# Base products of batches 2 and 3 taken as one seven-block product in the setup, and base and x remainders added by adding loads

## The chip, the cores and the metric

The kernel runs on one core of a Trainium2 chip. A core has five engines that work side by side, each on its own queue of instructions, in order: TensorE (PE in the profile) multiplies matrices, VectorE (DVE), ScalarE (ACT) and GpSimd (POOL) work elementwise, SyncE (SP) here only issues DMAs; ACT and POOL issue DMAs too. Engines wait for one another through semaphores. SBUF is the on-chip memory; PSUM holds what PE writes. The metric is device time in microseconds (us), lower is better, as the median of several executions.

## The reference, cut to what matters

There are 8 batches b, each of 1024 rows x of width 512. From cond, a low-rank update of the weights of layer 0 is computed (rank 8), and from weight, ys and d a modulated weight of layer 1:

```python
xw = gelu(layernorm(cond) @ w1 + b1) @ w2 + b2          # 8 x 8192
x_a, x_b = split(xw)                                     # 512 x 8 each, per batch
layer = base_layer + x_a @ x_b.T                         # per batch
x = x + (x + x @ layer)                                  # layer 0, with its residuals
ys = cond * scale; d = rsqrt((ys*ys) @ (w*w) + eps)      # per batch
out = x + ((x * ys) @ weight) * d                        # layer 1, with its residual
```

Both layers are linear in x, so the kernel multiplies x once by one 512x512 matrix per batch,

P(b) = (2 I + layer) @ N(b), with N(b) = I + diag(ys) weight diag(d).

The part (2 I + base) @ N(b) is called the base product; the rank term is added to it later.

## The kernel before

**Precision.** Products are made in fp32r, and each operand is held as a rounded part h and a remainder l (value minus h). A product takes three matmuls, h·h, h·l and l·h. Making a pair takes one ACT cast (`round_right`, L344; `round_b`, `split_p`, `split_x`) and one DVE subtraction (`rest`, L350), the latter after the former. ACT and DVE run through the helper at L62, so nearly all their profile lines say L62; all matmuls say L45, transposes L48. One reads the profile by tile names: nh and nl are the parts of N, bh and bl those of 2 I + base (held transposed), ph and pl those of P, xs those of x.

**Setup (to about 80 us).** While 16 MB of w2 stream in on SP's queue, PE multiplies each 1 MB tile by the gelu rows (`w2_group`, L389; products px), and between these fills itself with base products. N is made in halves of 256 rows by `n_half` (L333, DVE: per 128 rows one scale pass, and one small add of I on the diagonal block). Batch 0's base product is summed while weights arrive (`first_base`); those of batches 1, 2 and 3 are made by `Base` (L524): 16 steps of three matmuls for each of 4 row blocks' k chunks, so 48 matmuls of 128x512 for a batch, copied from PSUM to q by ACT. `Fill` (L695) runs these three one after another; `fill.make_n`, `fill.round` and `fill.finish` make, cast and subtract a half of N.

Between lie the rank steps: when px_1 is complete, `rank_t` (L435) makes `by`, transposes it (pb), multiplies it by the weight (pt_t) and selects rows with `stack` (L418; ps_t, then st_t). When px_0 is complete, `split(with_bias(0))` and `stack` make st_a from ps_a in the same way. P of batch 0 gets four rank products `rank_first` (L497; pr), which DVE adds to q_0, and `split_p` makes ph and pl of it.

**base itself.** base, transposed and with 2 I, lies in b_raw as the stationary operand. Batch 0's product is made with diag(ys) weight alone, without the I of N and without d; it is scaled by d first (`times_d`), so base, loaded as b_nat (1 MB, SP's queue), gets 2 I on its diagonal (`twice_i_plus_base`, L476) and is added to q_0 in four DVE passes (`add_base`, L481).

**Main stage (from about 80 us).** For batches 0 to 5, `main` (L811) multiplies 128 rows of x by P: 12 matmuls into po, copied and stored by ACT. Batches 4 and 5, and 6 and 7, get their base products in this stage as pairs (`Pair`, L547): with N's halves written [N1(b), N1(b+1); N2(b), N2(b+1)], a two-batch product of 2x2 blocks takes seven block products instead of eight (Strassen's scheme in Winograd's form; block p has right sums by `sums`, L562, and left operands from `left_sum`, L368, sums of b_raw's quarters). A `unit` (L611) is six matmuls, one of two row blocks of one p. Batches 6 and 7 use a like scheme for x (`Seven`).

**Order.** PE's matmuls are pinned to program order (L45). In the setup DVE, ACT and SP are pinned too (`InOrder`, L52, until `InOrder.on = False`), so the program text is the queue of each engine. In the main stage they are free, and a scheduler orders them.

**Buffers.** `big` has nine tiles of 1 MB for w2, x, q, b_raw, b_nat, the left sums' tile sraw and the xs; a load into one waits until the last reader of the tile that held it is done. nh and nl have two buffers each, n has four, and acc, the PSUM banks of base products, four.

The last part of the setup's text in the kernel before, with the order of the steps that the prediction follows:

```python
    fill.round(3, 0)
    fill.units(4)
    done = stack(xa, neg_a, "a", 0)
    fill.finish(3, 0)
    sa[0] = done()
    fill.units(3)
```

Of the kernel before, what the change touches and what calls it, by code (L numbers as in the profile page):

```python
# [7 lines left out]
F32 = mybir.dt.float32  # L8
F32R = mybir.dt.float32r
AF = mybir.ActivationFunctionType  # L10
ALU = mybir.AluOpType
# [19 lines left out]
def cond_resid_kernel(ctx: ExitStack, tc: tile.TileContext, small, cond, condrows, consts,  # L31
# [20 lines left out]
    class InOrder:  # L52
# [4 lines left out]
        def __init__(self, engine):  # L57
            self.engine = engine
# [20 lines left out]
    def big_tile(name, dtype=F32):  # L79
        return big.tile([P, KC, D], dtype, tag="big", name=name)  # L80
# [252 lines left out]
    def n_half(b, j):  # L333

        n = npool.tile([P, 2, D], F32, tag="n", name=f"n_{b}_{j}", bufs=4)
        for kk in range(2):
            k = 2 * j + kk
            ve.scalar_tensor_tensor(n[:, kk, :], w_sb[:, k, :], ysT[:, k, b:b + 1],
                                           d_all[b], ALU.mult, ALU.mult)
            blk = n[:, kk, k * P:(k + 1) * P]  # L340
            ve.tensor_add(blk, blk, ident)
        return n

    def round_right(n, name, wide=True):  # L344
# [20 lines left out]
    a11, a21 = b_raw[:, 0:2, 0:HD], b_raw[:, 0:2, HD:D]  # L365
    a12, a22 = b_raw[:, 2:4, 0:HD], b_raw[:, 2:4, HD:D]

    def left_sum(i):  # L368
        if i == 5:
            sraw["s"] = big_tile("sraw").rearrange("p k (u i) -> p k u i", u=2)  # L370
        s1, s2, s3, s4 = (sraw["s"][:, u] for u in range(4))
        s, x, y, op = {5: (s1, a21, a22, ve.tensor_add), 6: (s2, s1, a11, ve.tensor_sub),
                       3: (s4, a12, s2, ve.tensor_sub), 7: (s3, a11, a21, ve.tensor_sub)}[i]
        op(s, x, y)
        h = cp.tile([P, 2, HD], F32R, name=f"sh_{i}")
        l = cp.tile([P, 2, HD], F32R, name=f"sl_{i}")
        se.copy(h, s)
        ve.tensor_sub(l, s, h.bitcast(F32))
        left[i] = h, l

    b_nat = []


    px = [xps.tile([P, D], F32, name=f"px_{h}") for h in range(2)]
# [100 lines left out]
    def round_w(k):  # L485
        se.copy(wh[:, k, :], w_sb[:, k, :])
# [37 lines left out]
    class Base:  # L524
# [21 lines left out]

    class Pair:  # L547
# [144 lines left out]
    bcast_d(0)  # L692
    first_base(3, (1, 2, 3))

    class Fill:  # L695


        def __init__(self):
            self.bases = [Base(b) for b in (1, 2, 3)]
            self.ns, self.rests = {}, {}  # L700

        def units(self, count):
            for _ in range(count):
                if self.bases[0].at == 4 * KC:
                    self.bases.pop(0)
                self.bases[0].units(1)

        def make_n(self, b, j):
            self.ns[b, j] = n_half(b, j)

        def round(self, b, j):
            self.rests[b, j] = round_right(self.ns[b, j], f"{b}_{j}", b == 3)

        def finish(self, b, j):
            next(f for f in self.bases if f.b == b).add(self.rests[b, j]())

    fill = Fill()
    fill.make_n(1, 0)
    fill.round(1, 0)
    fill.make_n(1, 1)  # L720
    keep_first((0, 1))
    fill.round(1, 1)
    keep_first((2, 3))
    fill.finish(1, 0)
    for c in range(2):
        times_d(0, c)
    fill.finish(1, 1)
# [6 lines left out]
    fill.units(4)  # L734
    for k in range(2, KC):
        rest_w(k)
    fill.make_n(2, 0)
    w2_group()
    w2_group()
    fill.units(4)  # L740
    fill.round(2, 0)
    fill.make_n(2, 1)
    fill.finish(2, 0)
    w2_group()
    w2_group()
    fill.units(6)
    w2_group()
    steps = rank_t()
    next(steps)
    w2_group()  # L750
    next(steps)
    fill.units(4)
    w2_group()
    next(steps)
    w2_group()
    fill.units(2)
    fill.round(2, 1)
    next(steps)
    fill.finish(2, 1)
    next(steps)  # L760
    fill.units(3)
    twice_i_plus_base()
    w2_group()
    next(steps)
    w2_group()
    next(steps)
    mask_t()
    add_base(0)
    fill.units(2)
    fill.make_n(3, 0)  # L770
    next(steps)
    w2_group()
    w2_group()
    next(steps)
    fill.units(2)
    w2_group()
    load_x(0, 0)
    xa = (split(with_bias(0)),)
    fill.round(3, 0)
    fill.units(4)  # L780
    done = stack(xa, neg_a, "a", 0)
    fill.finish(3, 0)
    sa[0] = done()
    fill.units(3)
    fill.make_n(3, 1)
    p_tiles(0)
    rank_first(0)
    rank_first(1)
    fill.round(3, 1)
    fill.units(2)  # L790
    split_p(0, 0, 0)
    rank_first(2)
    rank_first(3)
    split_p(0, 0, 1)
    fill.finish(3, 1)
    split_p(0, 1)
    split_x(0, 0)
    fill.units(4)
    sa[1] = stack(xa, neg_a, "a", 1)()
    left_sum(5)  # L800
    fill.units(8)
    split_x(0, 1)
    for p in (6, 3, 7):
        left_sum(p)
    InOrder.on = False

    setup.close()
# [284 lines left out]
```

## Time and profile before

| | us |
|---|---|
| median of 3 executions | 302.23 (301.96 to 302.74) |
| profiled execution | 302.08 |
| its span | 300.3 |
| PE busy | 293.4 (98%), 1501 instructions |
| DVE busy | 211.0 (70%) |
| ACT busy | 154.1 (51%) |
| POOL busy | 34.8 (12%) |
| DMA | 62.14 MB, mean 207 GB/s |

The span is the time from the first to the last recorded instruction of one profiled execution; the device time has 1.8 us around it. The page divides the span into 40 slices of 7.5 us. A group's line gives engine, operation, output<-inputs, partitions x elements, count, busy time and mean, then the idle time ahead of it and what ended that. "PEld" is the load of a stationary operand, beside PE's matmuls. Matmuls are pipelined: one of 128x512 is recorded with about 0.39 us, but 12 in a row take 2.72 to 2.80 us in the chain that ended last. In timelines, a line is start, duration, engine, operation and tiles.

### The profile page before, as it was taken

Reading aid. Unit: us, or ns where it says so; the run is one execution under the profiler, and the core shown is the slowest. Engines: PE = TensorE matmul, PEld = TensorE weight load, DVE = VectorE, ACT = ScalarE, POOL = GpSimd, SP = SyncE. Lnnn points to the kernel's source line nnn. Section 1 sums busy time; section 2 is a strip of 40 time slices with the busy share of each in tenths; the row PEclk is TensorE's granted clock in tenths of the full one; section 3 lists DMA queues with packets and bytes.
Section 4 is the critical chain, followed back from the end, with each engine's and each line's share of the span. In section 5 each row is a group of like instructions: output and inputs, shape, how many; then the busy total and the mean of one; then the engine's idle time right before and its main releaser. Section 6 shows DMA issues by size and latency. Waiting matters only on the chain.

```text
span 300.3 us, 4005 instructions
## 1 busy us (share of the span) xinstructions
PE 293.4 (98%) x1501; PEld 227.1 (76%) x1501; DVE 211.0 (70%) x312; ACT 154.1 (51%) x226; POOL 34.8 (12%) x74
## 2 busy tenths in 40 slices
PE   7999999999999999999999999999999999999995
PEld 2655465466877778888887888888778888998995
DVE  4779840979569999935869994366562996479722
ACT  4757132256566673647634463656442663663630
POOL 0011000057004551000003600000000000000000
PEclk9999999999999999999999999999999999999999
DMA  7999999696619984605513841524516785131234
GB/s 210 410 428 419 405 424 419 219 326 183 197 70 305 306 288 126 239 35 210 204 43 97 230 164 46 201 55 192 210 70 210 244 267 227 38 140 49 93 140 142
DMA packets 19524, 62.14 MB, mean 207 GB/s; under 512 B 2720, under 2 KB 4000, under 8 KB 15152
## 3 DMA queue, kind: packets, MB, share of 16 engines
q1 hardware_dynamic: 6896, 39.57, 35.7%
q10 hardware_dynamic: 8832, 15.99, 14.2%
q0 software_dynamic: 3776, 6.31, 8.0%
q8 instruction: 12, 0.20, 0.3%
q14 instruction: 8, 0.07, 0.1%
HBM read 44.02 MB, written 17.84 MB: 206 GB/s over the span
## 4 chain that ended last, share of the span: by engine, by line
PE 84%; DVE 9%; ACT 3%; DMA 2%; issue 1%; SPq 0%; ACTq 0%
PE po L45 44%; PE pp L45 13%; PE pq L45 10%; PE sw L45 5%; PE px L45 4%; PE sz L45 2%; PE pg L45 2%; DVE n L62 2%; DMA b_raw<-in_baseT 2%; DVE sraw L62 1%; PE pr L45 1%; PE sv L45 1%; ACT o L62 1%; DVE sl L62 1%; ACT sh L62 1%
## 5 line engine op out<-in xcount | busy, mean ns | idle before, releaser
L45 PE MATMUL po<-ph,xs 128*128 128x512 f32 x384 | 123.8, 392 | 0.0
L45 PEld LDWEIGHTS po<-ph,xs 128*128 128x128 f32 x384 | 72.1, 188 | 16.8 <-issue 1.7
L45 PE MATMUL po<-pl,xs 128*128 128x512 f32 x192 | 74.8, 389 | 0.0
L62 ACT COPY o<-po 128x512 f32<-128x512 f32 x48 | 28.1, 586 | 52.8 <-PE po L45 52.8
L45 PEld LDWEIGHTS po<-pl,xs 128*128 128x128 f32 x192 | 36.1, 188 | 7.4
L62 DVE TENSOR_TENSOR xs<-x,xs 128x1024 fp32r<-128x1024 f32 x24 | 29.0, 1221 | 10.5 <-ACT xs L62 10.4
L62 ACT CAST xs<-x 128x1024 fp32r<-128x1024 f32 x24 | 24.9, 1052 | 3.7 <-DMA x<-in_x 1.9
L62 DVE TENSOR_TENSOR nl_p<-n,nh_p 128x1024 fp32r<-128x1024 f32 x14 | 17.1, 1222 | 12.3 <-ACT nh_p L62 12.2
L62 DVE TENSOR_TENSOR pl<-q,ph 128x1024 fp32r<-128x1024 f32 (+1 forms) x16 | 18.3, 1153 | 6.2 <-ACT ph L62 6.1
L62 DVE TENSOR_TENSOR q<-pr,q 128x512 f32<-128x512 f32 x32 | 20.1, 682 | 3.5 <-PE pr L45 3.5
L511 POOL DMA_DIRECT2D fa<-kept_a x28 | 13.7, 502 | 64.9 <-PE pr L45 64.8
L45 PE MATMUL pq<-nh,bh 128*128 128x512 f32 x48 | 19.8, 412 | 0.0
L45 PE MATMUL pq<-nl,bh 128*128 128x512 f32 x48 | 19.1, 398 | 0.1
L45 PE MATMUL pq<-nh,bl 128*128 128x512 f32 x48 | 19.0, 395 | 0.0
L62 DVE SCALAR_TENSOR_TENSOR n<-w_sb,ysT,d 128x512 f32<-128x512 f32 x24 | 17.7, 745 | 1.2 <-DMA d<-d_out 1.2
L62 ACT CAST nh_p<-n 128x1024 fp32r<-128x1024 f32 x14 | 14.8, 1054 | 6.3 <-PE pp L45 5.5
L62 ACT COPY o<-sw 128x512 f32<-128x512 f32 (+1 forms) x15 | 7.5, 500 | 19.2 <-PE sw L45 14.4
L62 ACT CAST ph<-q 128x1024 fp32r<-128x1024 f32 (+1 forms) x16 | 15.8, 1001 | 1.2 <-DVE q L62 0.8
L45 PE MATMUL px<-w,hT 128*32 128x512 f32 x128 | 16.0, 601 | 0.0
L62 ACT COPY q<-pp 128x512 f32<-128x512 f32 x20 | 11.7, 587 | 7.7 <-PE pp L45 7.7
L45 PEld LDWEIGHTS pq<-nh,bh 128*128 128x128 f32 x48 | 9.0, 188 | 8.4 <-issue 5.0
L511 POOL DMA_DIRECT2D ft<-kept_t x28 | 13.8, 509 | 5.2 <-DMA kept_t<-st_t 5.0
(185 smaller groups left out, 515.1 us busy)
## 6 DMA issues: line engine op xcount, KB each, us to landing
w<-in_w SPq DMA_DIRECT2D x16, 1024.0 KB, 10.5
x<-in_x SPq DMA_DIRECT2D x16, 1024.0 KB, 5.4
out<-o ACTq DMA_DIRECT2D x48, 256.0 KB, 3.2
out<-o ACTq DMA_DIRECT2D x6, 512.0 KB, 2.9
ft<-kept_t POOLq DMA_DIRECT2D x28, 64.0 KB, 3.4
fa<-kept_a POOLq DMA_DIRECT2D x28, 64.0 KB, 2.9
d<-d_out POOLq DMA_DIRECT2D x6, 256.0 KB, 5.2
w_sb<-in_weight SPq DMA_DIRECT2D x2, 512.0 KB, 5.3
```

Of the source, the lines that this page charges most:

```text
L45: tc.keep_in_program_order(nc.tensor.matmul(*args, **kw))
L62: return lambda *a, **kw: pin(f(*a, **kw)) if InOrder.on else f(*a, **kw)
L511: nc.gpsimd.dma_start(fold[name, b][32 * c:32 * c + 32, :], kept[name, g][32 * i:32 * i + 32, :])
```

## The change

Base products of batches 2 and 3 are no longer two `Base` of 48 matmuls each but one `Pair(2)` of 14 units of six, in the setup. Each unit's operands are made by the same calls in program order: `make_n`, `round` (right sum on DVE, cast on ACT) and `finish` (remainder on DVE). The left sums, made at the setup's end before, are made ahead of the units that need them, in two steps (`left_raw`, sum and cast; `left_rest`, remainder); b_raw is free after them.

base is not loaded to b_nat: `add_base` adds 2 I to q_0's diagonal blocks in one DVE pass, and a DMA on POOL's queue adds base from HBM to q_0 as it writes (`accum_op`). In the same way, the remainders of batch 0's x tiles 1 to 3 are not made by DVE: ACT writes -h, and a DMA on POOL's queue adds x from HBM to it. `n_half` adds I to both diagonal blocks in one pass.

```diff
@@ n_half
-            blk = n[:, kk, k * P:(k + 1) * P]
-            ve.tensor_add(blk, blk, ident)
+        blk = n.rearrange("p k (c i) -> p (k c) i", i=P)[:, 2 * j:2 * j + 6:5, :]
+        ve.tensor_add(blk, blk, ident.unsqueeze(1).to_broadcast([P, 2, P]))
@@ left sums
-    def left_sum(i):
+    def left_raw(i):
...
         h = cp.tile([P, 2, HD], F32R, name=f"sh_{i}")
+        se.copy(h, s)
+        sraw[i] = s, h
+
+    def left_rest(i):
+        s, h = sraw[i]
         l = cp.tile([P, 2, HD], F32R, name=f"sl_{i}")
-        se.copy(h, s)
         ve.tensor_sub(l, s, h.bitcast(F32))
@@ w2_group
-        if len(todo) == 6:
-            b_nat.append(big_tile("b_nat"))
-            sy.dma_start(b_nat[0], base)
@@ base added to q_0
-    def twice_i_plus_base():
-        for c in range(KC):
-            blk = b_nat[0][:, c, c * P:(c + 1) * P]
-            ve.scalar_tensor_tensor(blk, ident, 2.0, blk, ALU.mult, ALU.add)
-
-    def add_base(b):
-        for c in range(KC):
-            ve.tensor_add(q[b][:, c, :], q[b][:, c, :], b_nat[0][:, c, :])
+    def add_base():
+
+        blk = q[0].rearrange("p k (c i) -> p (k c) i", i=P)[:, 0:16:5, :]
+        ve.scalar_tensor_tensor(blk, ident.unsqueeze(1).to_broadcast([P, KC, P]), 2.0, blk,
+                                ALU.mult, ALU.add)
+        nc.gpsimd.dma_start(q[0], base, accum_op=ALU.add)
@@ split_x
-            ve.tensor_sub(xs[b, j][:, 1], t, xs[b, j][:, 0].bitcast(F32))
+            hi, lo = xs[b, j][:, 0], xs[b, j][:, 1]
+            if b == 0 and j:
+                se.mul(lo, hi.bitcast(F32), -1.0)
+                nc.gpsimd.dma_start(lo, x[b, j // 2][:, :, (j % 2) * 2 * P:(j % 2 + 1) * 2 * P],
+                                    accum_op=ALU.add)
+            else:
+                ve.tensor_sub(lo, t, hi.bitcast(F32))
```

The order of the setup's second half after the change, from the first w2 products behind base 1's first half (class `Fill` is gone; base 1 is `base1`, the pair is `two`):

```python
    two = Pair(2)
    two.make_n(1)
    w2_group(); w2_group()
    base1.units(4)
    two.round(1); two.make_n(2); two.finish(1)
    left_raw(5); left_raw(6)
    w2_group(); w2_group()
    base1.units(6)
    two.round(2); left_rest(5); left_raw(7); left_raw(3)
    w2_group(); steps = rank_t(); next(steps)      # by, and its cast
    left_rest(6)
    w2_group(); next(steps)                        # remainder of by
    left_rest(7); base1.units(2); two.finish(2); two.unit(); left_rest(3)
    w2_group(); next(steps)                        # pb
    two.make_n(5); two.round(5)
    w2_group(); two.unit(); next(steps)            # pt_t
    add_base(); two.finish(5); next(steps)
    two.units(2)
    w2_group(); next(steps); w2_group(); next(steps)
    mask_t(); two.unit(); two.make_n(6); next(steps); two.round(6)
    w2_group(); w2_group(); next(steps)
    two.unit(); two.finish(6)
    w2_group(); load_x(0, 0)
    xa = (split(with_bias(0)),)
    two.round(3); two.units(2)                     # product 6
    done = stack(xa, neg_a, "a", 0)                # ps_a0
    sa[0] = done()                                 # st_a0
    two.finish(3); two.round(7); two.unit()        # product 3, block 0
    p_tiles(0); rank_first(0); rank_first(1)
    two.unit()                                     # product 3, block 1
    split_p(0, 0, 0); rank_first(2); rank_first(3)
    split_p(0, 0, 1); split_p(0, 1)
    two.finish(7); split_x(0, 0)
    two.units(2)                                   # product 7
    two.round(4)
    sa[1] = stack(xa, neg_a, "a", 1)()
    two.finish(4); split_x(0, 1)
    two.units(2)                                   # product 4
```

(Several calls stand on one line here, and the comments on the right are the document's.)

More of the change, by code (lines that the diff above doesn't have):

```diff
@@ L375, in left_sum @@
         h = cp.tile([P, 2, HD], F32R, name=f"sh_{i}")
+        se.copy(h, s)
+        sraw[i] = s, h
+    def left_rest(i):
+        s, h = sraw[i]
         l = cp.tile([P, 2, HD], F32R, name=f"sl_{i}")
-        se.copy(h, s)
         ve.tensor_sub(l, s, h.bitcast(F32))
         left[i] = h, l
-    b_nat = []
     px = [xps.tile([P, D], F32, name=f"px_{h}") for h in range(2)]
@@ L693, in cond_resid_kernel, with round1 @@
     first_base(3, (1, 2, 3))
[L695 to L720, printed above, removed]
+    base1, n1 = Base(1), {}
+    def round1(j):
+        n1[j] = round_right(n1[j], f"1_{j}", False)
+    n1[0] = n_half(1, 0)
+    round1(0)
+    n1[1] = n_half(1, 1)
     keep_first((0, 1))
-    fill.round(1, 1)
+    round1(1)
     keep_first((2, 3))
-    fill.finish(1, 0)
+    base1.add(n1[0]())
     for c in range(2):
         times_d(0, c)
-    fill.finish(1, 1)
+    base1.add(n1[1]())
     for c in range(2, KC):
@@ L733, in cond_resid_kernel @@
         round_w(k)
-    fill.units(4)
+    base1.units(4)
     for k in range(2, KC):
         rest_w(k)
-    fill.make_n(2, 0)
+    two = Pair(2)
+    two.make_n(1)
     w2_group()
     w2_group()
[L740 to L743, printed above, removed]
+    base1.units(4)
+    two.round(1)
+    two.make_n(2)
+    two.finish(1)
+    left_raw(5)
+    left_raw(6)
     w2_group()
     w2_group()
-    fill.units(6)
+    base1.units(6)
+    two.round(2)
+    left_rest(5)
+    left_raw(7)
+    left_raw(3)
     w2_group()
@@ L749, in cond_resid_kernel @@
     next(steps)
+    left_rest(6)
     w2_group()
     next(steps)
-    fill.units(4)
+    left_rest(7)
+    base1.units(2)
+    two.finish(2)
+    two.unit()
+    left_rest(3)
     w2_group()
     next(steps)
+    two.make_n(5)
+    two.round(5)
     w2_group()
-    fill.units(2)
-    fill.round(2, 1)
+    two.unit()
     next(steps)
-    fill.finish(2, 1)
+    add_base()
+    two.finish(5)
     next(steps)
-    fill.units(3)
-    twice_i_plus_base()
+    two.units(2)
     w2_group()
@@ L767, in cond_resid_kernel @@
     mask_t()
-    add_base(0)
-    fill.units(2)
-    fill.make_n(3, 0)
+    two.unit()
+    two.make_n(6)
     next(steps)
+    two.round(6)
     w2_group()
@@ L774, in cond_resid_kernel @@
     next(steps)
-    fill.units(2)
+    two.unit()
+    two.finish(6)
     w2_group()
@@ L778, in cond_resid_kernel @@
     xa = (split(with_bias(0)),)
-    fill.round(3, 0)
-    fill.units(4)
+    two.round(3)
+    two.units(2)
     done = stack(xa, neg_a, "a", 0)
-    fill.finish(3, 0)
     sa[0] = done()
-    fill.units(3)
-    fill.make_n(3, 1)
+    two.finish(3)
+    two.round(7)
+    two.unit()
     p_tiles(0)
@@ L788, in cond_resid_kernel @@
     rank_first(1)
-    fill.round(3, 1)
-    fill.units(2)
+    two.unit()
     split_p(0, 0, 0)
@@ L794, in cond_resid_kernel @@
     split_p(0, 0, 1)
-    fill.finish(3, 1)
     split_p(0, 1)
+    two.finish(7)
     split_x(0, 0)
-    fill.units(4)
+    two.units(2)
+    two.round(4)
     sa[1] = stack(xa, neg_a, "a", 1)()
-    left_sum(5)
-    fill.units(8)
+    two.finish(4)
     split_x(0, 1)
-    for p in (6, 3, 7):
-        left_sum(p)
+    two.units(2)
     InOrder.on = False
```

## The prediction

> **What bounds the kernel now.** First the page: each engine's share, its 40 slices, and the chain that ended last.
>
> ```profile
> PE 293.4 (98%) x1501; PEld 227.1 (76%) x1501; DVE 211.0 (70%) x312; ACT 154.1 (51%) x226; POOL 34.8 (12%) x74
> ...
> PE   7999999999999999999999999999999999999995
> ...
> PE 84%; DVE 9%; ACT 3%; DMA 2%; issue 1%; SPq 0%; ACTq 0%
> ```
>
> PE is busy from the second slice to the last: what adds idle PE time adds span, what takes matmuls away may shorten it. The change lies between 33 and 92 us. Next, the busy time by 10 us stretch (columns PE, PEld, DVE, ACT, POOL, granted clock, DMA share, GB/s):
>
> ```profile
> 60.00:70.00 10.00, 10.00 (x51) 6.60 (x44) 8.10 (x14) 4.22 (x7) 5.07 (x10) 1.00 0.84 289
> 70.00:80.00 10.00, 9.78 (x41) 7.28 (x40) 9.06 (x12) 6.28 (x9) 5.57 (x11) 1.00 0.70 210
> ```
>
> PE has no hole while DVE is 81 to 91% busy, so PE runs through only because matmuls with ready operands lie between its waits. The timelines of this stretch show how (start, duration):
>
> ```profile
> 62.37 1.06 PE L45 MATMUL px<-w,hT 128*32 128x512 f32 x8
> ...
> 66.25 0.40 PE L45 MATMUL ps_a<-work,sel 128*128 128x512 f32 x1
> ```
>
> ```profile
> 63.50 0.69 DVE L62 TENSOR_TENSOR scr<-px,rows 128x512 f32<-128x512 f32 x1 [0.58 <-PE px L45]
> 64.94 0.75 DVE L62 SCALAR_TENSOR_TENSOR work<-work,cst,scr 128x512 fp32r<-128x512 f32 x1 [0.74 <-ACT work L62]
> 65.88 1.23 DVE L62 TENSOR_TENSOR nl<-n,nh 128x1024 fp32r<-128x1024 f32 x1 [0.19 <-ACT nh L62]
> 67.36 0.75 DVE L62 SCALAR_TENSOR_TENSOR st_a<-work,cst,ps_a 128x512 fp32r<-128x512 f32 x1 [0.25 <-ACT work L62]
> ...
> 72.49 1.22 DVE L62 TENSOR_TENSOR pl<-q,ph 128x1024 fp32r<-128x1024 f32 x1
> 73.62 1.22 DVE L62 TENSOR_TENSOR nl<-n,nh 128x1024 fp32r<-128x1024 f32 x1
> 74.76 1.22 DVE L62 TENSOR_TENSOR pl<-q,ph 128x1024 fp32r<-128x1024 f32 x1
> ```
>
> The remainder nl is made before st_a, which waits for ps_a; the next nl stands between the two pl. Both are ready long before PE needs them. Last, the DMA issues of the w2 stream:
>
> ```profile
> 57.01 0.33 SPq L62 DMA_DIRECT2D w<-in_w  x1
> 60.05 0.33 SPq L62 DMA_DIRECT2D x<-in_x  x1
> ```
>
> **What the Trainium skill says.** "PSUM — Partial Sum Buffer", Engine vs sequencer instructions: the ScalarE and VectorE queues are strict FIFO, and matmuls start in program order. The trace agrees: pr at 71.34 waits for DVE's q sums while later matmuls had their operands. "TensorE: Matmul & The Clock Gate", Part 1, What's actually happening: after an idle window of about 3.4 us PE's clock halves until a busy window has passed. No run shows it here: the granted clock is 1.00 throughout and the longest hole behind the warm-up 0.6 us. "DMA: Bandwidth & Descriptors", SWDGE vs HWDGE vs iDMA: an accumulating DMA can only be issued by GpSimd; the trace has none. Its section Anatomy of one DMA gives 2.0 us plus bytes at 436 GB/s, so 4.4 us for 1 MB and 3.2 us for 512 KB, estimates. The trace has 5.3 us for the idle-time 1 MB x load, so the page is too low here.
>
> **The change part by part.** The built program's order on each engine says what follows what; durations are from the timelines of before. A 128x512 matmul follows the last by 0.232 us (12 in 2.78). A DVE 128x1024 pass takes 1.22 and its successor starts 1.14 after it, 128x512 0.69/0.60 (0.75/0.66 with a scalar), ACT's cast 1.05/0.95 and 0.62/0.52, its PSUM copy 0.59/0.49. A waiting engine starts 0.03 to 0.08 after its releaser.
>
> *Taken away.* Batches 2 and 3 took 2x48 matmuls; seven products, two row blocks, six matmuls each make 84. PE has 12 fewer: -12x0.232 = **-2.8 us**. PE's present waits for DVE at pr 2 and pr 3 go too, since larger ones stand there: the matmul before them starts at 70.22, they at 70.74 and 71.34, 0.29 and 0.37 behind the rhythm of 0.232 (**-0.6**). The diagonal add in one pass saves about 0.2 us of DVE per half; the four q+b_nat passes (2.5 us) and b_nat's 1 MB on SP's queue go; all of it is under PE, hence nothing.
>
> *SP's queue.* With the left sums' tile early, six w2 loads start 1 to 5 us later (their buffers are those of w2 tiles read at 20.8, 25.8, 31.0 us and so on), and those after 43 us earlier: the last w2 issues at about 48.7, not 57.01. At the stream's 420 GB/s, 2.5 us per tile, the tightest (w2_0_0_0, issued 32.3, landing about 39, read at 42.1) keeps 3 us. Nothing.
>
> *Stall 1, the transposes pb.* ACT's nh for product 2 reuses the buffer that base 1's last unit reads; this unit is now first on PE after 43.00 and ends 44.67. ACT stands there, and behind it sh_7, sh_3 and the cast work<-by: 44.71 + 0.95 + 0.52 + 0.52 = 46.70, done 47.32, DVE's work 47.35 to 48.10, pb 48.15 instead of 46.99: **+1.2**. PE stands behind pb, so the w2 products, product 1's second block and pt_t all move by it. Then product 2 has twelve matmuls where nine stood (+0.7, counted in the 84), and the second matmul of ps_t0 waits 0.1 for DVE's remainder of t (57.25). The last w2 product starts at 62.37 + 1.2 + 0.7 + 0.1 = 64.34. Product 6 follows: DVE makes its right half from st_t0 on (58.37) and ends its nl at 64.99, while PE needs it at 65.67: free, by 0.7.
>
> *Stall 2, product 3.* ps_a0 stands 12 matmuls behind the last w2 product as before (66.25 - 62.37 = 3.88), so it starts at 68.22. In DVE's queue nl of product 3 now stands behind st_a0. ACT: two copies of product 6 end 69.00, cast of ps_a0 68.90 to 69.49; st_a0 69.52 to 70.27; nl 70.18 to 71.40. PE's second matmul of product 3 was due at 68.69, starts 71.45: **+2.8**. Behind it on PE: everything.
>
> *Stall 3, product 7.* Its nl now stands behind both pl passes of P. From 71.45 PE runs the rest of block 0, pr 0 and 1, block 1 and pr 2 and 3 by about 75.1; q sums on DVE to 76.58; ph on ACT 76.61 to 77.66; the second pl 77.69 to 78.91; nl 78.83 to 80.05. PE was due at 75.33: **+4.8**.
>
> *Stall 4, product 4.* Product 7's last matmul starts 80.10 + 10x0.232 = 82.43; ACT copies it by 83.46; DVE adds 83.49 to 84.18, then makes the right sum of product 4 (84.09 to 85.31); ACT casts 85.34 to 86.39, then ps_a1 to 86.88; st_a1 to 87.66; nl 87.57 to 88.79. PE starts 88.84 instead of 83.13: **+5.7**. Eleven matmuls (2.55) end the setup, and the first main product starts at about 91.4, where before it started at 80.35.
>
> Sum: 1.2 + 0.1 + 2.8 + 4.8 + 5.7 - 2.8 - 0.6 = 11.2; by the clock 91.4 - 80.35 = **+11.05**. PE is gapless from there, so nothing is given back.
>
> *Clock.* Holes of 4.6 us and of 5.8 us (with one matmul in it) exceed the page's window. Bounds: 0 (the windows fall badly, twice) to 3.4 (two windows at half speed, 1.7 each). Windows that run freely fit into them with chances of (4.6-3.4)/3.4 = 0.35 and 0.7, so 1.8 us in the mean if a lone matmul counts as idle; I take 1.5.
>
> *Adding loads.* Base: issued about 55.6, q_0's next reader on DVE at 73.4; it costs nothing unless it takes over 17 us. The x remainders: the first is issued at about 89 behind ACT's negation, needed 97.5 by the third matmul of tile 2; 1 MB of x starts beside it at 88, when ACT has read the buffer that it takes. From 5.3 us per MB alone to twice the traffic: 4 to 10 us, so 0 to +1.5 us; I take 0. The next two have 8 and 13 us. DVE loses three passes of 1.22 there, ACT gains three of 1.05 at a time when it is half idle: nothing.
>
> Against the profiled execution's 302.08 (span 300.3 and 1.8 around it): 302.1 + 11.05 + 1.5 = 314.6; the median, 302.23, is 0.15 above it: **314.7 us**.
>
> **Rivals.** *A: gapless PE, the other side.* Only the matmuls count: 302.2 - 2.8 - 0.6, about 299. For it: PE is the bound and DVE and ACT have idle time. Against it: order in a queue, not idle time, makes the stalls. It decides if the four stalls together come to less than 3.4 us, that is if each nl is done when PE arrives. Chance 0.05; 0.02 more for a tie. *B: only half the stalls.* Products 3 and 7 stall but the chain of product 4 is shorter than I add up, or the first stall makes room for later ones: 305 to 310. Chance 0.12. *C: the adding loads land late*, beside the stalls. Each accumulates in SBUF, by a rate that no row shows; from 8.5 us on they hold tile 2 and then tile 4: 317 to 322. Chance 0.13. My forecast, 311 to 317: 0.68. That 12 matmuls go is certain from the program.
>
> **Range.** 309 to 319 leaves out A, the tie, the low end of B and the top of C, about 2 in 10. A difference below 0.3% is no difference here. Faster 0.05, same 0.02, slower 0.93.
>
> **What would show it.** PE holes of about 1.2 us before pb, 2.8 before the second matmul of product 3, 4.6 in product 7 and 5.8 ahead of product 4, each ended by DVE (pb by work, the others by nl_p); PE busy falling from 100% to about 60% between 68 and 90; the first main product near 91 to 93; 12 fewer matmuls; a clock below 1.00 only behind the holes. I am wrong if the holes end on a DMA, if ACT doesn't wait for PE before pb, or if PE is gapless there.

## The result, and the profile after

The changed kernel takes 317.85 us (median of 6 runs, 317.15 to 319.82) against 302.46 us (301.86 to 302.86), a ratio of 1.052 with a 95% interval of 1.049 to 1.055. It is slower by 15.4 us; forecast were 314.7 us and a range of 309 to 319. Here and in the experiments the median and the range in brackets are over all runs, and the ratio leaves out runs more than 1.5% above the fastest of the same kernel. The profiled execution of the changed kernel took 319.82 us, with a span of 318.0 us; the other five lie 1.3 to 2.7 us below it.

The page of the changed kernel, with the rows that were shown of the kernel before:

```profile
PE 297.7 (94%) x1489; PEld 229.0 (72%) x1489; DVE 215.3 (68%) x299; ACT 159.8 (50%) x232; POOL 39.4 (12%) x78
...
PE   8999988986539999999999999999999999999995
...
PEclk9999999997578999999999999999999999999999
...
PE 82%; DVE 6%; DMA 5%; ACT 3%; issue 2%; SPq 1%; ACTq 0%; DVEq 0%
```

PE has its 12 matmuls fewer (1501 to 1489), and is nevertheless busy for 4.3 us longer, since some of the matmuls ran at half clock. The loss lies in four of the forty slices, from about 70 to 95 us, and there the granted clock dips as well. By stretches of 10 us (columns PE, PEld, DVE, ACT, POOL, granted clock, DMA share, GB/s):

```profile
60.00:70.00 10.00, 10.00 (x56) 5.60 (x52) 7.33 (x10) 5.18 (x8) 1.64 (x3) 1.00 1.01 296
70.00:80.00 10.00, 5.59 (x17) 4.07 (x16) 7.54 (x10) 3.50 (x5) 5.08 (x10) 0.83 0.77 249
80.00:90.00 10.00, 5.36 (x12) 3.81 (x12) 6.06 (x7) 2.45 (x4) 3.90 (x8) 0.66 0.24 52
```

Before, PE was busy for 9.78 and 10.00 of the 10 us behind 70 and behind 80. No engine is full here: DVE fell from 9.06 to 7.54 in the stretch from 70 us. They wait for each other. PE's waits in the trace (total, times, longest):

```profile
PE pp L45 <- DVE nl_p L62: 8.8, 3, 4.6
PE pp L45 <- ACT nh_p L62: 3.4, 1, 3.4
PE pb L48 <- DVE work L62: 1.1, 1, 1.1
PE px L45 <- DMA w<-in_w: 1.0, 1, 1.0
```

In time they stand so on PE (start, duration, in brackets the hole ahead and what ended it):

```profile
43.34 1.06 PE L45 MATMUL px<-w,hT 128*32 128x512 f32 x8 [1.02 <-DMA w<-in_w]
...
49.55 0.66 PE L48 MATMUL pb<-sm,work 128*128 128x128 f32 x4 [1.15 <-DVE work L62]
...
72.66 0.50 PE L45 MATMUL pp<-nl_p,sh 128*128 128x512 f32 x1 [2.62 <-DVE nl_p L62]
...
74.99 0.63 PE L45 MATMUL pp<-nl_p,sh 128*128 128x512 f32 x1
75.42 0.63 PE L45 MATMUL pp<-nh_p,sl 128*128 128x512 f32 x1
...
82.78 0.80 PE L45 MATMUL pp<-nl_p,sh 128*128 128x512 f32 x1 [4.57 <-DVE nl_p L62]
...
91.51 0.79 PE L45 MATMUL pp<-nh_p,bh 128*128 128x512 f32 x1 [3.38 <-ACT nh_p L62]
93.91 0.80 PE L45 MATMUL pp<-nl_p,bh 128*128 128x512 f32 x1 [1.61 <-DVE nl_p L62]
...
98.46 0.40 PE L45 MATMUL po<-ph,xs 128*128 128x512 f32 x1
```

All four stalls are where they were forecast. There is one hole more, ahead of 43.34, for a w2 tile. From 74.6 us on matmuls follow each other by 0.43 us instead of 0.23 (74.99 to 75.42). The last line is the first main product, which started at 80.35 before: 18.1 us later. The timelines of ScalarE and VectorE give the reasons, to be held against the one shown of before:

```profile
46.10 1.05 ACT L62 CAST nh_p<-n 128x1024 fp32r<-128x1024 f32 x1 [4.15 <-PE pq L45]
48.74 0.75 DVE L62 SCALAR_TENSOR_TENSOR work<-work,cst,by 128x512 fp32r<-128x512 f32 x1 [4.33 <-ACT work L62]
...
66.69 0.69 DVE L62 TENSOR_TENSOR scr<-px,rows 128x512 f32<-128x512 f32 x1 [0.24 <-PE px L45]
68.12 0.75 DVE L62 SCALAR_TENSOR_TENSOR work<-work,cst,scr 128x512 fp32r<-128x512 f32 x1 [0.74 <-ACT work L62]
70.72 0.75 DVE L62 SCALAR_TENSOR_TENSOR st_a<-work,cst,ps_a 128x512 fp32r<-128x512 f32 x1 [1.85 <-ACT work L62]
71.39 1.22 DVE L62 TENSOR_TENSOR nl_p<-n,nh_p 128x1024 fp32r<-128x1024 f32 x1
...
79.17 2.42 DVE L62 TENSOR_TENSOR pl<-q,ph 128x1024 fp32r<-128x1024 f32 x2
81.50 1.22 DVE L62 TENSOR_TENSOR nl_p<-n,nh_p 128x1024 fp32r<-128x1024 f32 x1
...
88.49 0.69 DVE L62 TENSOR_TENSOR q<-q,q 128x512 f32<-128x512 f32 x1 [1.87 <-ACT q L62]
89.10 1.22 DVE L62 TENSOR_TENSOR n<-n,n 128x1024 f32<-128x1024 f32 x1
```

For stall 1, ScalarE stands 4.15 us at nh_p of product 2 until base 1's last matmuls are done, and VectorE then waits for the cast of by behind it; only after that can pb start. Further on, nl_p of product 3 stands behind st_a, for which VectorE is idle for 1.85 us, and nl_p of product 7 behind both pl. For stall 4, the right sum of product 4 (n, at 89.10) stands behind the sums of q, which wait for ScalarE's copy of product 7. Before, nl stood ahead of st_a and between the two pl.

The adding loads, of which before shows none (KB each, us from issue to landing):

```profile
xs<-in_x POOLq DMA_DIRECT2D x3, 512.0 KB, 7.6
...
q<-in_base POOLq DMA_DIRECT2D x1, 1024.0 KB, 12.6
```

PE waits for neither.

**Where the time went.** By the trace, from one kernel's first main product to the other's: the four stalls come to 1.15 + 2.8 + 4.7 + 5.6 = 14.3 us (each from the time at which the matmul was due to its start, product 4 without what the clock adds), the w2 tile to 1.0, the half clock to about 5.9 (some 30 matmuls by 0.195 us each, in three stretches that lose 1.6, 2.3 and 2.0 us). The matmuls saved and the waits at pr take 3.4 off. Together 17.8, of the 18.1 that the starts show. This execution is the longest of the six and has the lowest mean clock (0.973; the others 0.978 to 0.984), so its clock term is above the typical one.

### The profile page after: what moved, and what is told of

The parts are those of the page before. It is cut to its first block, busy times and chain, and to the rows that moved or that the text cites. A ratio compares the mean times of both kernels' runs of the same rounds, so it can differ in the third digit from the quotient of the medians.

```text
span 318.0 us, 3984 instructions
## 1 busy us (share of the span) xinstructions
PE 297.7 (94%) x1489; PEld 229.0 (72%) x1489; DVE 215.3 (68%) x299; ACT 159.8 (50%) x232; POOL 39.4 (12%) x78
## 4 chain that ended last, share of the span: by engine, by line
PE 82%; DVE 6%; DMA 5%; ACT 3%; issue 2%; SPq 1%; ACTq 0%; DVEq 0%
PE po L45 42%; PE pp L45 20%; PE sw L45 6%; DMA w<-in_w 3%; PE sz L45 3%; PE px L45 3%; PE pg L45 3%; DMA b_raw<-in_baseT 2%; PE pq L45 1%; PE sv L45 1%; PE pr L45 1%; DVE nl_p L62 1%; DVE q L62 1%; DVE pl L62 1%; SPq L62 1%
## 5 line engine op out<-in xcount | busy, mean ns | idle before, releaser
L62 DVE TENSOR_TENSOR xs<-x,xs 128x1024 fp32r<-128x1024 f32 x21 | 25.4, 1221 | 19.2 <-ACT xs L62 19.1
L62 DVE TENSOR_TENSOR nl_p<-n,nh_p 128x1024 fp32r<-128x1024 f32 x21 | 25.7, 1222 | 16.1 <-ACT nh_p L62 16.1
L62 ACT CAST nh_p<-n 128x1024 fp32r<-128x1024 f32 x21 | 22.1, 1052 | 25.8 <-DVE n L62 15.7
L62 ACT COPY q<-pp 128x512 f32<-128x512 f32 x30 | 17.6, 586 | 20.4 <-PE pp L45 20.3
L45 PE MATMUL pp<-nl_p,sh 128*128 128x512 f32 x48 | 20.4, 425 | 7.2 <-DVE nl_p L62 7.2
L45 PE MATMUL pp<-nh_p,sh 128*128 128x512 f32 x48 | 20.2, 422 | 0.0
L45 PE MATMUL pp<-nh_p,sl 128*128 128x512 f32 x48 | 20.1, 420 | 0.0
L45 PE MATMUL pp<-nh_p,bh 128*128 128x512 f32 x36 | 15.5, 430 | 3.4 <-ACT nh_p L62 3.4
L62 DVE SCALAR_TENSOR_TENSOR n<-w_sb,ysT,d 128x512 f32<-128x512 f32 x24 | 17.0, 746 | 0.7 <-DMA d<-d_out 0.7
L45 PEld LDWEIGHTS pp<-nl_p,sh 128*128 128x128 f32 x48 | 9.8, 205 | 10.0 <-DVE nl_p L62 8.1
```

What stands on the lines that cost most here:

```text
L45: tc.keep_in_program_order(nc.tensor.matmul(*args, **kw))
L62: return lambda *a, **kw: pin(f(*a, **kw)) if InOrder.on else f(*a, **kw)
```

## The experiments

The theory: order in the queues of VectorE and ScalarE makes the four stalls, the holes halve the clock, and neither the seven products nor the adding loads cost anything by themselves. Rivals: the adding loads are what is late; the holes are one backlog of VectorE, which only moves from place to place.

### 1. The clock, by filling the holes

Zero matmuls into a bank that nothing reads any more stand in the holes ahead of products 3, 7 and 4; all else is the changed kernel.

```diff
     two.round(7)
+    filler(12)
     two.unit()
@@
     split_x(0, 0)
+    filler(20)
     two.units(2)
@@
     split_x(0, 1)
+    filler(24)
     two.units(2)
```

> The changed kernel with 12, 20 and 24 extra matmuls of zeros into a PSUM bank that is no longer used, ahead of product 3, of product 7 and of product 4, where PE stands idle. No wait is changed and no result. Theory: a part of the loss is the clock, which halves in the holes; filled holes keep it at 1.00, the waits stay, and the time falls from 317.9 to 313 to 314.5 us. Rival: PE is waiting in those stretches anyway, so a slower clock costs nothing: 317 to 318.5, with the clock at 1.00.

Measured: 313.59 us (312.75 to 314.33), ratio 1.037 (1.034 to 1.039), granted clock 1.00. With the same queues and the same VectorE work, 4.3 us go when only the clock stays up: that is what the half clock costs in the median, shown apart from the waits. Up to 0.5 us of it may be the w2 tile of 43 us, for which PE waits 0.52 us in this trace and not 1.02.

### 2. Stall 2 alone

```diff
-    sa[0] = done()
     two.finish(3)
+    sa[0] = done()
```

> The changed kernel with one DVE instruction moved: the remainder of product 3 stands ahead of st_a0 and no longer behind it. Theory (order within DVE's queue makes the holes): the hole ahead of product 3's second matmul, 2.6 us, goes and the rest moves up by it: 315.2, or down to 312.5 if the clock then drops later too. Rival (DVE is short of time as a whole, so a hole that is closed reopens further on): 317 to 318.

Measured: 315.11 us (314.68 to 316.71), ratio 1.043 (1.040 to 1.046): 2.7 us less, for one line of order. The waits for nl_p fall from 8.8 us in three to 6.5 in three; the longest is still 4.5.

### 3. Stall 3 alone

```diff
     two.round(7)
+    two.finish(7)
     two.unit()
@@
     split_p(0, 1)
-    two.finish(7)
     split_x(0, 0)
```

> The changed kernel with one line moved: VectorE's remainder of right 7 ahead of its rank sums of q_0 and both passes of pl, instead of behind them. Theory (stall 3 is that queue position, nothing else): ScalarE's rounding of right 7 is done at 74.9 in the trace of the changed kernel, so product 7 no longer waits and the 4.6 us ahead of it go; but the next link of the chain, the right sum of product 4, stands behind pl, the remainder of x and the sums of q_3 in VectorE's queue, and moves up less than product 7 does: product 4 begins at 87 to 88 instead of 91.5, 313.3 to 315. Rival (the holes are one and the same slack, VectorE's backlog, so that what goes at product 7 comes back in full at product 4): 317 to 318.5.

Measured: 314.53 us (313.44 to 315.38), ratio 1.041 (1.039 to 1.042): 3.3 us less, in the range of the theory; product 4 begins a little earlier than it said (85.57, not 87 to 88). PE's line of this kernel, the holes behind stall 2:

```profile
76.23 1.10 PE L45 MATMUL pr<-tm,st_a 128*128 128x512 f32 x2 [1.43 <-DVE q L62]
85.57 0.80 PE L45 MATMUL pp<-nh_p,bh 128*128 128x512 f32 x1 [3.67 <-ACT nh_p L62]
87.97 0.79 PE L45 MATMUL pp<-nl_p,bh 128*128 128x512 f32 x1 [1.61 <-DVE nl_p L62]
```

The 4.6 us ahead of product 7 are gone; 1.4 came back at the next pr, whose bank waits for the q sums that now stand behind nl_p, and 0.3 at product 4. So the holes aren't one backlog that moves on in full, but a line moved forward in a queue delays what it overtakes.

### 4. Stall 4 alone

Product 4 leaves the setup and is computed behind tile 1 of batch 0.

```diff
-    two.round(4)
     sa[1] = stack(xa, neg_a, "a", 1)()
-    two.finish(4)
     split_x(0, 1)
-    two.units(2)
+    two.round(4)
+    two.finish(4)
@@
+    at(0, 1, two.units, 2)
```

> The changed kernel with the two units of product 4 moved out of the setup, behind tile 1 of batch 0 in the main stage; its right sum is still made in the setup. Theory (stall 4 is TensorE waiting at product 4 for a right sum that is late by a chain of ScalarE and VectorE work, and nothing else needs that time): the waits pp<-nh_p 3.4 and pp<-nl_p 1.6 go, with half or so of the 4.3 us that the clock costs, since the hole ahead of product 4 is the largest that is left but one: 5.0 + 2.0 off, 309.5 to 312.5. Rival (the main stage could not have begun before anyway, for the split of P or of x): the waits turn into waits of the first main product of the same length and the time stays above 315.

Measured: 314.18 us (314.04 to 315.18), ratio 1.040 (1.039 to 1.042). That is 3.7 us less, not the 5.3 to 8.3 expected. Product 4 waits no more, but PE's line has, in its place:

```profile
87.80 0.50 PE L45 MATMUL po<-ph,xs 128*128 128x512 f32 x1 [1.82 <-DVE st_a L62]
```

The first main product does not read st_a. Its PSUM tile does take a bank of the setup's, and these are free only when VectorE has read ps_a1 into st_a, which now ends 0.1 us ahead of it (experiment 8 moves that read and the wait goes). So the rival was right for 1.8 us: something else stood close behind stall 4. The granted clock is 0.984, as in half of the changed kernel's runs, so the clock gave little or nothing back.

### 5. The adding loads

Base by a plain load and four passes of VectorE, the remainders of x on VectorE, as before the change; the seven products stay.

```diff
     def add_base():
-        blk = q[0].rearrange("p k (c i) -> p (k c) i", i=P)[:, 0:16:5, :]
-        ve.scalar_tensor_tensor(blk, ...)
-        nc.gpsimd.dma_start(q[0], base, accum_op=ALU.add)
+        twice_i_plus_base()
+        for c in range(KC):
+            ve.tensor_add(q[0][:, c, :], q[0][:, c, :], b_nat[0][:, c, :])
@@
-            if b == 0 and j:
+            if False:
@@ and the load of b_nat on SyncE's queue, as before
```

> The changed kernel with both adding loads undone: base comes as b_nat by SP's queue and is added in four DVE passes, and the three x remainders are made by DVE. Theory: the adding loads cost nothing where they are; DVE, which is 99% busy from 50 to 60 us, gets 2.7 us more to do there, so the second matmul of ps_t0 waits longer: 319 to 321. Rival (the adding loads are part of the loss): 312 to 317.

Measured: 322.71 us (318.77 to 324.71), ratio 1.063 (1.056 to 1.069); its profiled execution is the shortest, 318.77. It is not faster without them, so they aren't the cause; the median is even above the 319 to 321 expected. In the trace the waits for nl_p (8.8 us in three) and nh_p (3.4) are as in the changed kernel, and one is there that the changed kernel has not:

```profile
PE ps_t L45 <- DVE work L62: 2.3, 1, 2.3
```

The remainder of t stands behind the passes over base in VectorE's queue. In this order of the setup the adding load of base does relieve VectorE.

### 6. The w2 stream and stall 1

First base 1 finished early, so that ScalarE's rounding for product 2 need not wait for base 1's last unit:

```diff
-    base1.units(6)
+    base1.units(8)
@@
     left_rest(7)
-    base1.units(2)
```

> The changed kernel with the last two steps of batch 1's base product ahead of the w2 products of tiles 1_1_3 and 0_0_0, not behind them. The nh buffer for product 2 is then free early, and tile 0_0_0 is needed 1.4 us later. Theory: the waits at pb (1.15 us) and at px for w2 (1.0 us) go: 315.7. Rival (product 7's and 4's chains set the end, whatever happens ahead of them): 317.5 to 318.

Measured: median 321.77 us (318.65 to 324.26), ratio 1.055 (1.053 to 1.057): no gain. Its two shorter runs, 318.65 and 319.64 us, are still above the theory's 315.7 and the rival's 318. The profiled execution, 323.9 us, is 5 us above the shortest, so the sizes of its waits aren't used here.

Then the left sums in place, in blocks of b_raw, without the tile sraw:

```diff
-        if i == 5:
-            sraw["s"] = big_tile("sraw").rearrange("p k (u i) -> p k u i", u=2)
-        s1, s2, s3, s4 = (sraw["s"][:, u] for u in range(4))
+        s1, s2, s3, s4 = a22, a11, a21, a12
@@ and 5, 7, 6, 3 as the order of the sums
```

> The changed kernel with the four left sums written in place, into blocks of b_raw that no later sum reads, so that the tile sraw goes and the w2 stream gets its buffer back (order of the sums 5, 7, 6, 3). Theory (the buffer that sraw took is what makes TensorE wait 1.0 us for a w2 tile, because SyncE stands before the issue of 0_1_0 until a buffer comes free): that wait goes, SyncE issues the w2 tile after 0_0_0 several microseconds earlier than 44.5, and the time falls by about 1 us, to 316.4 to 317.2. Rival (the DMA engines were the limit, not the buffer): the wait for w2 stays at about 1 us or moves to a later tile, and the time stays at 317.5 to 318.5.

Measured: 318.02 us (317.41 to 318.03), ratio 1.052 (1.050 to 1.053). Half a hit. The wait for w2 has gone, and from 24 to 36 us the w2 stream runs at 331 to 422 GB/s, by windows of 4 us, where the changed kernel has 294 to 320, so the buffer was its cause. (The size of that wait varies: in the traces of experiments 1 to 4, which all keep sraw, it is 0.2 to 1.2 us.) The time hasn't moved. The clock is 0.973 in three of its four runs and 0.973 to 0.984 in those of the changed kernel; in the two traces at 0.973 the spans are 316.1 and 318.0. The gain is smaller than what the clock makes of a few us of holes from run to run, and isn't shown by the times.

Last, both:

> The changed kernel with two edits of before at once: left sums in place (the w2 stream keeps its buffer) and base 1 finished early (ScalarE's rounding for product 2 no longer waits for base 1's last unit). Each alone gave nothing or a loss. Theory (base 1 early takes stall 1 away, but brings the w2 products forward, and with sraw's buffer missing from the stream the tiles were late for it; with the buffer back they are in time): neither pb nor px waits, the 1.1 us of stall 1 go for good, 316 to 317.3. Rival (the w2 stream is limited by the DMA engines, which share the time with base's adding load, so the tiles are late in any case): waits for w2 of 1 to 4 us behind 60 us, 318 to 320.

Measured: 320.79 us (317.80 to 322.42), ratio 1.062 (1.059 to 1.065): the rival, and a little above its 318 to 320. The waits at pb and at 43 us are gone, and PE stands at the last w2 product instead:

```profile
66.19 1.07 PE L45 MATMUL px<-w,hT 128*32 128x512 f32 x8 [3.38 <-DMA w<-in_w]
```

That tile was asked for by 50.2 us. The windows of this trace say why it came so late (same columns as above, last two DMA share and GB/s):

```profile
48.00:50.00 2.00, 2.00 (x11) 1.41 (x8) 2.00 (x4) 0.02 (x1) 0.00 (x0) 1.00 0.14 33
...
60.00:62.00 2.00, 2.00 (x16) 0.84 (x9) 1.89 (x2) 0.75 (x2) 0.90 (x2) 1.00 1.02 283
```

The DMA engines are almost idle from 48 to 50 us, as SyncE issued no tile from 44 to 48 us. They are full afterwards, but from 58 to 66 us move only 246 to 295 GB/s while base's adding load (issued 54.25, landed 12.8 us later) runs beside the tile; from 52 to 56 us the stream made 414 to 418. Whether it is the adding load that holds the tile up, experiment 10 tests.

### 7. All orders mended

In-place sums and base 1 early as above, and a new end of the setup. Its core:

```python
    two.round(3)
    src = with_bias(0)
    hi, rest_a = work_tile(), work_tile()
    se.copy(hi, src)
    two.finish(3)                     # between ScalarE's rounding and VectorE's remainder
    ve.scalar_tensor_tensor(rest_a, hi.bitcast(F32), neg_u, src, ALU.mult, ALU.add)
    two.n[7] = two.sums(7)
    ...                               # product 6, ps_a0
    two.round(7); sa[0] = done(); two.finish(7)
    two.unit(three); two.unit(three)  # product 3, its sums into q_3 held back
    ...                               # pr, product 7, split of P and of x 0_0
    two.n[4] = two.sums(4); two.round(4)
    split_x(0, 1, 1); two.finish(4)
    three[0](); three[1](); flush_adds()
```

Product 4 is behind tile 1; tiles 0 and 1 run together, all products of ph with the rounded x first.

> The changed kernel with the orders mended all at once: left sums in place; base of batch 1 finished early; the right half of batch 3 made at once where VectorE waits for the bias; VectorE's remainder of right 3 between ScalarE's rounding of the x rows and VectorE's own, its remainder of right 7 ahead of the rank sums of q_0; the sums of q_3 held back until P is split; product 4 behind tile 1; tiles 0 and 1 of batch 0 together, the products of the rounded parts first; the remainder of x tile 0_1 on VectorE, not by an adding load. The arithmetic of the results is the same. Theory (all of the loss is order: stalls 1 to 4, the clock that they cost and the w2 buffer; none of it is in the seven products or the adding loads): TensorE runs nearly without holes at full clock, the first main product starts at 76 to 78, product 4 costs its 2.8 us later, 299 to 303, so level with the kernel before or faster. Rival (the work itself is too long for VectorE in this stage: its queue is full from 48 us on): holes of 3 us or more stay ahead of product 7 or of the first main product, 304 to 309.

Measured: 304.76 us (304.49 to 304.85), ratio 1.008 (1.007 to 1.010). Of the 15.4 us, 13 are back, with the same seven products and the same adding load of base. But the time is in the rival's range, 304 to 309, not in the theory's, and as the rival had it a hole of over 3 us stands ahead of the first main product, which starts at 78.83, not at 76 to 78. Besides pb's it is the only one left in the stage, and it is the bank that experiment 4 met; the last read of it, st_a, stands in VectorE's queue behind both pl:

```profile
78.83 2.76 PE L45 MATMUL po<-ph,xs 128*128 128x512 f32 x8 [3.59 <-DVE st_a L62]
```

### 8. The second stack earlier

```diff
     done = stack(xa, neg_a, "a", 0)
+    done1 = stack(xa, neg_a, "a", 1)
     two.round(7)
@@
     sa[0] = done()
+    sa[1] = done1()
@@ and the right half of batch 3 behind the remainder of by,
@@ product 6's second copy behind the rounding of right 7
```

> The mended kernel before this one, with two more lines of order changed. (1) The second stack of x rows is done behind the first, where VectorE waits 0.7 us for ScalarE's rounding of right 7, not after P is split: the main stage's PSUM tiles take the banks of the setup's, so its first product waited 3.6 us for VectorE's last read of the second stack. (2) The right half of batch 3 is made behind the remainder of the x rows for the transposes, not ahead of it. Theory: the waits po<-st_a 3.6 and pb<-work 1.1 go, with about 1 us of half clock: 304.8 - 3.6 - 1.1 - 1 = 299, taken 298.5 to 300.5, faster than the kernel before. Rival (the first main product then waits for the split of P instead, which ends on VectorE at 78.1 in that trace): only part of the 3.6 us goes, 301 to 303.5, level with the kernel before.

Measured: 305.16 us (302.39 to 307.19), ratio 1.006 (1.004 to 1.009): both waits went, the first main product started at 74.45, and no time was won: forecast were 298.5 to 300.5 and, by the rival, 301 to 303.5. PE's waits:

```profile
PE po L45 <- DMA xs<-in_x: 3.3, 2, 3.0
PE px L45 <- DMA w<-in_w: 1.1, 1, 1.1
```

The forecast's rival C, adding loads that land late, has come true here: with the main stage 24 us earlier than in the changed kernel, the adding loads of x (6.0 and 12.8 us) no longer have cover.

### 9. The remainders of x on VectorE

```diff
-            if b == 0 and j > 1:
+            if False:
```

> The mended kernel before this one, with the adding loads of x undone: VectorE makes the remainders of x tiles 0_2 and 0_3, as the kernel before does. Base is still added by an adding load. Theory (with the holes of the setup gone the main stage comes 20 us earlier than in the changed kernel, and the adding loads of x, 6.0 and 12.8 us from issue to landing, are what it now waits for: 0.3 and 3.0 us, with half clock behind the second): these waits and the half clock go, VectorE has room for two passes of 1.22 us each between 83.7 and 90.0 us, 299.5 to 301.5, faster than the kernel before by about 0.5%. Rival (the wait is for the bytes of x or for buffers, not for the adding): the x loads themselves are late, and waits for them or for ScalarE of 2 us or more take the place, 302 to 304.

Measured: 300.65 us (299.76 to 305.65), ratio 0.996 (0.995 to 0.998): as expected, now ahead of the kernel before. The wait for the last w2 tile is left (1.6 us).

### 10. Base's adding load later

```diff
-    add_base()
     two.finish(5)
@@
     two.unit()
+    add_base()
     two.make_n(6)
```

> The mended kernel of 300.65 us with base's adding load asked for some 6 us later: behind the mask of the rank factor, ahead of the right half of batch 3, so that the last w2 tile has less of it beside it. Theory (the w2 wait of 1.6 us that is left at 64.5 is that tile sharing the DMA engines with the adding load, which takes 13.3 us from issue to landing): the wait goes or falls below 0.5 us, the adding load, alone with one x tile, lands in 8 to 11 us, by 71, as q_0 is read next at 71 to 72: 299 to 300. Rival (the adding load takes 13 us wherever it stands): it lands at 73 or later, TensorE waits 1 to 3 us for the rank sums of q_0, 300.5 to 303.

Measured: 299.44 us (299.31 to 299.92), ratio 0.991 (0.989 to 0.993). The wait for w2 is gone, which shows that the adding load held the tile up: SyncE issued the last w2 tile at 51.6 in both kernels, and only the adding load moved, from 54.4. The adding load was now issued at 59.35 and landed after 11.7 us, not the 8 to 11 expected. Its reader on VectorE waits 0.28 us for it, PE not at all:

```profile
71.18 1.29 DVE L62 TENSOR_TENSOR q<-pr,q 128x512 f32<-128x512 f32 x2 [0.28 <-DMA q<-in_base]
```

The page of this kernel, to be held against those of before and of the change:

```profile
PE 291.2 (98%) x1489; PEld 225.0 (76%) x1489; DVE 218.6 (73%) x302; ACT 157.1 (53%) x229; POOL 35.7 (12%) x75
...
PE   8999999999899999999999999999999999999995
...
PEclk9999999999999999999999999999999999999999
```

PE's longest wait behind the warm-up is 0.8 us. The kernel takes 2.7 us less than the kernel before beside it (302.14), close to the 12 matmuls' 2.8. That these 2.7 us are the worth of the seven products is read from the sizes only: the two kernels differ in other things too.

## Why the prediction was right or wrong

**Right:** sign, range and cause. The changed kernel loses to four stalls, each ended by the instruction named, at the place named. The number alone would not have shown it: 317.85 us lies above the prediction's main band (311 to 317; its own terms add up to 314.8, not 314.7) and in the one that it gave to rival C, 317 to 322. What decides is that no wait of PE ends on an adding load, and experiment 5. From due time to start:

| step | predicted, us | trace, us |
|---|---|---|
| The 12 matmuls | -2.8 | 12 fewer; the whole kernel is 2.7 us faster once nothing waits (experiment 10) |
| Waits at pr | -0.6 | none left |
| Stall 1, pb | +1.2 | 1.15 |
| Stall 2, product 3 | +2.8 | 2.8, and 2.7 by undoing it |
| Stall 3, product 7 | +4.8 | 4.7 |
| Stall 4, product 4 | +5.7 | 5.6 |
| SP's queue | 0 | 1.0 |
| Clock | +1.5 (0 to +3.4) | 4.3 by filling the holes, about 5.9 in the profiled run |
| Adding loads | 0 | no wait |

The first main product, forecast near 91 to 93, started at 98.46, 18.1 us later than before: that is 11.05 as forecast, 1.0 for the w2 tile and about 5.9 for the clock.

**Clock** is the term that was mis-sized. With the 1.0 us of SP's queue it makes up the 3.1 us between 314.7 and 317.85 (3.8 by these figures, which are of different runs). The step let the clock fall only for a hole longer than a window of about 3.4 us, and each time for one window at most. Read in steps of 0.1 us, the granted clock of the trace is 0.50 in three stretches, from 74.2 to 77.6, from 81.0 to 87.8 and from 91.3 to 98.1 us: 3.4 us once and 6.8 us twice, and all six edges lie on one grid of 3.41 us. By the windows of this grid:

| window, us | PE busy in it, us | clock in it |
|---|---|---|
| 67.4 to 70.8 | 2.7 | 1.00 |
| 70.8 to 74.2 | 1.5 | 1.00 |
| 74.2 to 77.6 | 3.4 | 0.50 |
| 77.6 to 81.0 | 0.6 | 1.00 |
| 81.0 to 84.4 | 1.7 | 0.50 |
| 84.4 to 87.8 | 3.4 | 0.50 |
| 87.8 to 91.3 | 0.3 | 1.00 |
| 91.3 to 94.7 | 1.6 | 0.50 |
| 94.7 to 98.1 | 3.4 | 0.50 |
| 98.1 to 101.5 | 3.4 | 1.00 |

The clock of each window follows from how busy PE was in the window before it. The ten traces of this document that show half clock all fit such a grid. From 30 us on, behind a window at full clock with 1.53 us of work or less the next was at half clock in every case (17); behind one with 1.97 us or more it never was; between 1.56 and 1.88 us both occurred. At half clock, 1.9 us of work or less kept the clock down, and 3.0 us or more brought it back; nothing lay between. So a hole needn't fill a window, and if PE resumes late in a window, the next one is slow too: this is what the bound of 3.4 us left out. In the Trainium skill, "TensorE: Matmul & The Clock Gate", Part 1, What's actually happening, from which the step drew its window, the window is also said to run freely, not from the kernel's start. The traces agree: the hole of 2.6 us ahead of product 3 stands in seven of them and is followed by half clock in two, in which 1.88 us of it or more fall into one window; in the other five it is 1.84 us at most. What that page calls an idle window had, here, up to 1.5 us of work in it. The mean clocks of the six runs, 0.984, 0.978 and 0.973, are by estimate three, four and five windows of 3.41 us at half clock in 316 us.

**SP's queue** took the margin of one tile, w2_0_0_0, at the stream's 420 GB/s. With fewer buffers the stream itself ran at 294 to 320 GB/s from 24 to 36 us; the tile landed 10.6 us after its issue at 32.72, not some 7, and PE waited 1.0 us. That is the one hole that ended on a DMA. The last w2 issue, put at 48.7, was at 52.8, behind a wait of SyncE for sraw's buffer. Experiment 6 took PE's wait away with the buffer.

**Adding loads** cost nothing in this kernel, as said, but by cover and not by size: base took 12.6 us against the prediction's estimate of 4.4, within the 17 us that the step allowed. (The plain load of 5.3 us that the prediction compared with its estimate ran on SyncE's queue, the adding load on GpSimd's.) Experiments 8 and 9 show the price where the cover is gone: 3.3 us for x, 1.1 to 1.6 for base, through the w2 tile beside it. The step's bound of 4 to 10 us for x was too low at the top (12.8 in experiment 8).

**The rivals.** A, gapless PE at about 299 us, is what experiment 10 reaches, with another order; the change as made is far from it. B, half the stalls, is out: all four came in full. C is out for the changed kernel, though the time lies in its band (experiment 5), and came true in experiment 8.

**Left open:** with both edits of experiment 6 the trace, at 317.8 us, is the shortest of five runs; the others take 2.8 to 4.6 us more. Their mean clocks are 0.973 and 0.968 against its 0.984, two or three windows at half clock more, each worth up to 1.7 us (an estimate). That is enough for the difference, but no trace of them shows it. Base 1 early alone left no profile whose waits could be sized.

## What to carry to other kernels

Where PE is full and the others seem to have room, cost a change by the order in each in-order queue: for every operand that PE needs, ask what it stands behind, and what that in turn waits for; here the place of four remainders and roundings cost five times what 12 matmuls gave. Allow for half clock behind every hole from some 2.6 us on, for 3.4 or 6.8 us of it, and expect it to come in some runs and not in others. For a stall that is taken away ask what stands close behind it: a PSUM bank, an x tile and a w2 tile each came up as the next. An adding load takes work from VectorE, but here 1 MB of it took some 12 us or more; look at which load shares the DMA engines with it.

## What was not expected of the hardware

- Half clock came in whole windows of 3.41 us, one or two at a time, on a grid that holds through a trace. A hole of 2.6 us was enough where it left no more than 1.5 us of work in one window, and in another trace (experiment 6, both edits) one of 3.4 us was not. At half clock, matmuls followed each other by 0.43 us instead of 0.23.
- An adding load of 1 MB took 11.7 to 13.3 us wherever it stood, one of 512 KB 5.9 to 12.8 us; a plain load of 1 MB of the same x took 5.3 us when little else ran. With one of 1 MB under way in the changed kernel (60 to 68 us), the DMA engines were at a share of about 1.0 but moved 270 to 295 GB/s, against 420 of the plain w2 stream. A load of x and transfers of the rank factors and of d ran at the same time, so how much of this is the adding load isn't shown.
